# The node matrix beside conv 1's node product, and a new order of the steps, in a two-layer graph network

## The chip, the cores and the metric

The kernel runs on one core of a Trainium2 chip. The metric is device time in microseconds for the whole program, the median of several runs. One execution of it was profiled; times below in the form "at 1212.13 us" are counted from that execution's first instruction. The engines are PE (TensorE), DVE (VectorE), ACT (ScalarE), POOL (GpSimd) and SP (SyncE, which here only issues transfers).

## The reference

There are 128 graphs of 128 nodes with 512 features. Each goes through two layers, each with a layer norm and relu ahead and a residual sum behind.

```python
h = relu(layernorm(x))
# layer 0: two hypergraph convolutions with the same graph
H = (adj != 0); w = adj[0, :]
conv(h, W, b) = Dinv * (H @ (Binv * (H.T @ (h @ W.T)))) + b    # D = H @ w, B = H.sum(0)
r = layer_norm(relu(conv(h, W1, b1)))                         # 512 -> 1024
x = x + conv(r, W2, b2) + h                                    # 1024 -> 512
# layer 1: mean aggregation
h = relu(layernorm(x))
agg = (adj @ h) / max(adj.sum(-1), 1e-6)
x = x + relu(concat(h, agg) @ W.T)
```

## The kernel before

**Tiling.** One graph fills the 128 partitions with its nodes, so a graph is the unit of work. H (B^-1) H^T is a 128 x 128 matrix of the graph alone, the *node matrix*; it is made once and used in both convolutions. It comes from one matmul with 258 columns (`node_matrix`, L428 to L433, into `ps_s`): the columns hold H^T scaled by the high and by the low part of B^-1, and two columns more for D. ACT copies the first half out with a factor (L432), and DVE adds the second half (`node_sum`, L436 to L438). The result is `s`.

**Split products.** The weight products run as fp32r matmuls on operands split in high, low and difference parts. `product` (L521 to L537) opens two PSUM banks, a main one for high and low, and one for the difference: 12 matmuls of 512 columns for 512 inputs (8 and 4), 24 for 1024. Per graph that is `conv1_weights` for each half of the 1024 outputs (`rm`, `rd`, 24 in all), `conv2_weights` (`gm`, `gd`, 24), `layer1_mean` (`bm`, `bd`, 12) and `layer1_self` (`am`, `ad`, 12). With conv 2's node product (`conv2_nodes`, `ym`, `yd`, 3) and `aggregate` (3 into `am`, `ad`) this makes 78 matmuls of 512 columns a graph. Conv 1's node product (`conv1_nodes`, L485 to L489, into `pz`) is in plain fp32: four products of 128 columns, which show as eight matmuls.

**What lies between the products.** ACT writes the high part of each split operand and the main results; DVE writes low and difference parts, adds the difference results, and does all 32 x 32 block transposes. Full transposes go through DRAM: `inner_out` and `inner_in` write conv 1's normalised result `r` (512 KB) and read it back in blocks, four transfers; `inner_turn` transposes the blocks on DVE. `layer1_trip_out`, `layer1_trip_in`, `layer1_turn` do that for layer 1's input, `mean_out`, `mean_in`, `mean_transpose` for the scaled adjacency matrix.

**Order.** The whole order is written out by hand: `head()` for the first graphs, `step(s)` (L856 to L943) for s = 3 to 124, `tail()` for the rest. A step works on eight graphs at once, from `load_adjb` of graph s + 3 and `incidence` of s + 2 to `finish` and `store` of s - 4. Each engine takes its instructions in this order, and so does SP with its transfers; semaphores make an instruction wait for what it reads and for the buffer that it writes. A step on PE is: `node_matrix(s + 1)`, `conv1_weights(s, 1)`, `conv2_nodes(s - 2)`, `layer1_mean(s - 3)`, `conv1_nodes(s + 1)`, `layer1_self(s - 3)`, `conv2_weights(s - 1)`, `aggregate(s - 3)`, `conv1_weights(s + 1, 0)`.

**Stages.** The decorator `stage` (L115 to L124) drops a call whose graph lies outside 0 to 127, or which the set `done` already holds. So calls in `tail()` that were made earlier vanish.

**Buffers.** Most SBUF tags have one buffer, and several tags are shared: `t1` by the turned `r`, its difference part and conv 2's node parts; `t2` by the blocks read back and the low part; `t3` by the high part and conv 2's `gp`; `r` by conv 1's result of one graph after the other, which `inner_out` still reads; `junk` by `inner_spread`'s waste and by the output `o`, which `store` reads; `adj` by one graph's adjacency matrix, which `mean_out` reads. Six PSUM banks turn among the weight products, conv 2's node product and the like (`bank`), and two among `ps_s` and `pz` (`small_bank`, L109). The matrices `s` have four buffers.

**Lines that the steps below touch:** small scalings run on the engine that the call names, through `scaled` (L296 to L300: L298 on ACT, L300 on DVE and POOL); sums and differences through `combine` (L76 to L81), on POOL in halves of 256 columns; layer norms through `sums`, `spread`, `scales`, `shifts`, `normalise` (L304 to L326) under the names `x_...`, `inner_...`, `layer1_...`. `conv1_out` is L555, `inner_turn` and `layer1_turn` are L591, all high parts L612, all difference parts L621, `conv2_main` L690, `conv2_weights_out` L694, `conv2_high` L706, `node_high` L717, `conv2_out` L754, `layer1_self_out` L838, `finish` L844 (L847 for the last graphs), `store` L853.

## Time and profile before

| what | value |
|---|---|
| median of 3 runs | 2447.64 us (2446.86 to 2447.76) |
| the profiled execution's own time | 2447.67 us |
| its span, first to last instruction | 2445.9 us |
| granted TensorE clock | full (1.0) |
| PE matmul busy, instructions | 2422.7 us, 11170 |
| DVE busy, instructions | 2298.1 us, 5843 |
| ACT busy, instructions | 2009.9 us, 4512 |
| POOL busy, instructions | 1324.8 us, 1808 |
| DMA | 311.39 MB, mean 127 GB/s |
| spacing of node matrices on PE, steady steps | median 18.747 us |

A group's line gives the source line, the engine and operation, what it writes from what, how often, its busy time and mean length, and the idle time of its engine just before it with what ended it. A matmul's end is modelled and overlaps the next one's start, so on PE starts are compared. Instructions on DVE and ACT overlap their neighbours a little too, so the distance from start to start is some 80 or 100 ns less than a length.

### The profile page before, as it was taken

How to read it: one execution, taken by the hardware profiler on the slowest of the kernel's cores; microseconds unless marked ns; L12 is line 12 of the kernel's file. 1: busy time of each engine (PE TensorE's matmuls, PEld its weight loads, DVE VectorE, ACT ScalarE, POOL GpSimd, SP SyncE). 2: the span in 40 equal slices, each digit the busy share in tenths (PEclk: the TensorE clock that was granted, in tenths of full speed). 3: DMA queues.
4: the chain of work that ended last, by engine and by line, in shares of the span. 5: the costliest groups of instructions: out<-in, count | busy, mean ns of one | idle time of the engine just before them, and what ended most of it. 6: DMA issues, size and time to landing. Idle time of an engine off the chain costs nothing.

```text
span 2445.9 us, 41647 instructions
## 1 busy us (share of the span) xinstructions
PE 2422.7 (99%) x11170; PEld 2009.6 (82%) x11170; DVE 2298.1 (94%) x5843; ACT 2009.9 (82%) x4512; POOL 1324.8 (54%) x1808
## 2 busy tenths in 40 slices
PE   7999999999999999999999999999999999999998
PEld 5788888888888888888888888888888888888886
DVE  8899999999999999999999999999999999999987
ACT  8888888888888888888888888888888888888785
POOL 5555555555555555555555555555555555555552
PEclk9999999999999999999999999999999999999999
DMA  6344433344434443444344443434343444344432
GB/s 186 114 129 125 130 124 129 124 130 128 129 119 130 132 126 123 129 129 127 124 128 128 126 129 123 132 123 130 122 133 121 130 127 131 119 131 131 127 124 92
DMA packets 408956, 311.39 MB, mean 127 GB/s; under 512 B 176656, under 2 KB 339984, under 8 KB 408720
## 3 DMA queue, kind: packets, MB, share of 16 engines
q1 hardware_dynamic: 407888, 308.66, 40.1%
q8 instruction: 88, 1.44, 0.2%
q14 instruction: 148, 1.21, 0.2%
q10 hardware_dynamic: 576, 0.07, 0.0%
q0 software_dynamic: 256, 0.01, 0.0%
HBM read 166.21 MB, written 142.34 MB: 126 GB/s over the span
## 4 chain that ended last, share of the span: by engine, by line
PE 95%; ACT 2%; DVE 1%; DMA 1%; issue 1%; SPq 0%; POOL 0%; POOLq 0%; DVEq 0%; ACTq 0%
PE gm L530 19%; PE rm L530 18%; PE am L530 9%; PE bm L530 9%; PE gd L535 9%; PE rd L535 9%; PE bd L535 5%; PE ad L535 5%; PE pz L488 4%; PE am L832 2%; PE ad L832 1%; PE ym L743 1%; PE yd L744 1%; PE ym L742 1%; PE ps_s L430 1%
## 5 line engine op out<-in xcount | busy, mean ns | idle before, releaser
L306 ACT ACTIVATE h<-x_t 128x512 f32<-128x512 f32 x255 | 159.1, 624 | 291.8 <-DVE x_t L754 283.8
L81 POOL TENSOR_TENSOR r<-r,b_bc 128x256 f32<-128x256 f32 x500 | 358.7, 739 | 70.1 <-DVE r L555 54.4
L300 POOL TENSOR_SCALAR st<-st 128x1 f32<-128x1 f32 x130 | 82.3, 633 | 569.9 <-DVE st L317 563.2
L81 POOL TENSOR_TENSOR hl<-ht,hh 128x256 fp32r<-128x256 f32 x250 | 235.4, 963 | 216.5 <-ACT hh L612 216.5
L81 POOL TENSOR_TENSOR x_t<-x_t,h 128x256 f32<-128x256 f32 x256 | 239.8, 959 | 1.3 <-ACT h L326 1.1
L81 POOL TENSOR_TENSOR g<-g,c 128x256 f32<-128x256 f32 x246 | 177.6, 743 | 72.4 <-DVE g L694 72.4
L326 ACT ACTIVATE h<-x_t,st 128x512 f32<-128x512 f32 x255 | 206.1, 808 | 2.0 <-POOL st L300 1.2
L555 DVE SCALAR_TENSOR_TENSOR r<-rd,dinv,r 128x512 f32<-128x512 f32 x256 | 190.8, 746 | 7.7 <-ACT r L550 6.3
L81 POOL TENSOR_TENSOR x_t<-x_t,b_bc 128x256 f32<-128x256 f32 x256 | 187.2, 752 | 0.0
L311 ACT ACTIVATE h<-x_t,st 128x512 f32<-128x512 f32 x255 | 182.9, 717 | 4.1
L550 ACT ACTIVATE r<-rm,dinv 128x512 f32<-128x512 f32 x256 | 174.7, 684 | 7.7 <-PE rm L530 4.4
L694 DVE SCALAR_TENSOR_TENSOR g<-gd,g 128x512 f32<-128x512 f32 x127 | 87.8, 691 | 79.5 <-issue 70.4
L621 DVE SCALAR_TENSOR_TENSOR nd<-nh,nl 128x1024 fp32r<-128x1024 f32 x127 | 155.5, 1225 | 4.2
L326 ACT ACTIVATE r<-r,st 128x1024 f32<-128x1024 f32 x128 | 157.8, 1233 | 0.1
L591 DVE STREAM_TRANSPOSE nt<-nb 128x1024 f32<-128x1024 f32 x127 | 156.9, 1235 | 0.4 <-DMA nb<-n_scratch 0.3
L81 DVE TENSOR_TENSOR nl<-nt,nh 128x1024 fp32r<-128x1024 f32 x127 | 153.5, 1208 | 1.9 <-ACT nh L612 1.7
L530 PE MATMUL am<-w31h,hh 128*128 128x512 f32 x504 | 146.8, 413 | 0.0
L311 ACT ACTIVATE junk<-r,st 128x1024 bf16<-128x1024 f32 x128 | 145.2, 1134 | 0.1
L488 PEld LDWEIGHTS pz<-s,h 128*128 128x128 f32 x1024 | 134.5, 192 | 11.1 <-ACT h L326 0.7
L530 PE MATMUL rm<-w11h,z 128*128 128x512 f32 x512 | 140.3, 396 | 0.0
L530 PE MATMUL rm<-w11l,z 128*128 128x512 f32 x512 | 139.3, 393 | 0.0
L530 PE MATMUL rm<-w10h,z 128*128 128x512 f32 x512 | 138.2, 392 | 0.9 <-ACT z L501 0.9
(244 smaller groups left out, 7594.1 us busy)
## 6 DMA issues: line engine op xcount, KB each, us to landing
n_scratch<-r SPq DMA_DIRECT2D x128, 512.0 KB, 2.6
nb<-n_scratch SPq DMA_DIRECT2D x508, 128.0 KB, 2.8
x_t<-in_x_dram SPq DMA_DIRECT2D x128, 256.0 KB, 2.7
h_scratch<-h SPq DMA_DIRECT2D x127, 256.0 KB, 2.3
hb<-h_scratch SPq DMA_DIRECT2D x508, 64.0 KB, 1.9
out_dram<-o SPq DMA_DIRECT2D x127, 256.0 KB, 2.0
adj_t<-in_adj_dram SPq DMA_DIRECT2D x128, 64.0 KB, 1.9
an_scratch<-adj_t SPq DMA_DIRECT2D x128, 64.0 KB, 1.6
```

The lines of the kernel that those rows point to most:

```text
L81: eng.tensor_tensor(dst[:, s], a[:, s], b[:, s], op)
L306: copy(junk, src, func, accum_out=t[:, 0:1])
L311: copy(junk, src, AF.Square, bias=t[:, 1:2], accum_out=t[:, 2:3])
L326: copy(dst, src, func, bias=t[:, 5:6], scale=t[:, 4:5])
L488: nc.tensor.matmul(z[:, k * P : (k + 1) * P], H0[g][:, k * P : (k + 1) * P], S[g], start=True, stop=True)
L530: nc.tensor.matmul(pm, left[i](k), right(i, k), start=(i == 0 and k == 0), stop=(i == 1 and k == kk - 1))
L535: nc.tensor.matmul(pd, left[2](k), right(2, k), start=(k == 0), stop=(k == kk - 1), skip_group_check=True)
L550: copy(R[g][:, HALVES[half]], PY.pop((g, half)), AF.Copy, scale=DN[g][:, 1:2])
L555: nc.vector.scalar_tensor_tensor(r, PR.pop((g, half)), dn[:, 0:1], r, MUL, ADD)
L591: nc.vector.transpose(nt.rearrange("p k (i b) -> p k i b", b=B), t.rearrange("p i k a -> p k i a"))
L621: nc.vector.scalar_tensor_tensor(t, h, 2.0**-12, low, MUL, SUB)
L694: nc.vector.scalar_tensor_tensor(G[g], PG.pop(g), 4096.0, G[g], MUL, ADD)
```

## The change

`node_matrix` becomes a thin stage around a plain function `matrix`. For graphs 4 to 125 `conv1_nodes(g)` calls `matrix(g + 1)` ahead of its own matmuls, and marks that stage as done; the call of `node_matrix` is gone from `step`, and the one for graph 126 in `tail` vanishes. In step s, `conv1_nodes(s + 1)` so makes the matrix of graph s + 2, one graph earlier than before; `node_sum` moves to s + 2 with it. The stages of `step` come in a new order. PE's is now: `conv1_weights(s, 1)`, `conv2_nodes(s - 2)`, `layer1_mean(s - 3)`, `layer1_self(s - 3)`, then the matrix of s + 2 and `conv1_nodes(s + 1)`, `conv2_weights(s - 1)`, `aggregate(s - 3)`, `conv1_weights(s + 1, 0)`. SP's is: `inner_out`, `mean_out`, `load_adj`, `inner_in`, `mean_in`, `store`, `layer1_trip_out`, `load_adjb`, `load_x`, `layer1_trip_in`. Some stages change their engine: `node_floor`, `conv1_bias(s, 0)` and `shifts(s, 2)` go from POOL to DVE; `incidence_weight`, `incidence_scale(s + 2, 1)` and `shifts(s + 2, 1)` from DVE to ACT; `incidence_scale(s + 2, 0)` and `mean_scale` from DVE to POOL. `head` and `tail` are unchanged.

```diff
--- before.py
+++ after.py
@@ -424,8 +424,7 @@
         c = SPLIT["sb", g][i]
         scaled(eng, SB[g][:, i * (P + 1) : i * (P + 1) + P], HT[g], c)
 
-    @stage
-    def node_matrix(g):
+    def matrix(g):
         PS[g] = ps = small_bank("ps_s")
         nc.tensor.matmul(ps[:, : 2 * P + 2], HT.pop(g), SB.pop(g)[:, : 2 * P + 2], start=True, stop=True)
         s = small.tile([P, P + 1], FP, tag="s", name="s", bufs=4)
@@ -433,6 +432,10 @@
         S[g] = s
 
     @stage
+    def node_matrix(g):
+        matrix(g)
+
+    @stage
     def node_sum(g):
         s = S[g]
         nc.vector.scalar_tensor_tensor(s, PS.pop(g)[:, P + 1 : 2 * P + 2], 4096.0 if steady(g) else 1.0, s, MUL, ADD)
@@ -483,6 +486,9 @@
 
     @stage
     def conv1_nodes(g):
+        if 4 <= g <= N - 3:
+            done.add((node_matrix.f, g + 1))
+            matrix(g + 1)
         PZ[g] = z = small_bank("pz")
         for k in range(KD):
             nc.tensor.matmul(z[:, k * P : (k + 1) * P], H0[g][:, k * P : (k + 1) * P], S[g],
@@ -854,93 +860,92 @@
 
 
     def step(s):
+        incidence(s + 2)
+        conv2_bias(s - 2)
+        inner_out(s - 1)
         node_high(s - 2)
-        conv2_bias(s - 2)
+        conv1_weights(s, 1)
+        mean_out(s - 3)
+        layer1_high(s - 3)
+        node_rest(s - 2)
         conv2_high(s - 2)
+        incidence_count(s + 2, nc.vector)
+        conv1_main(s, 0)
+        incidence_weight(s + 2, nc.scalar)
+        node_floor(s + 1, nc.vector)
+        load_adj(s - 2)
         layer1_self_main(s - 4)
-        layer1_high(s - 3)
-        inner_out(s - 1)
+        inner_in(s - 1)
+        x_norm(s + 1)
+        incidence_inverse(s + 2)
         conv2_low(s - 2, nc.vector)
-        x_norm(s + 1)
-        node_rest(s - 2)
-        conv1_main(s, 0)
+        conv1_out(s, 0)
+        conv2_rest(s - 2)
+        layer1_low(s - 3)
+        conv2_nodes(s - 2)
+        conv1_main(s, 1)
+        layer1_rest(s - 3)
+        conv2_out(s - 2)
+        incidence_high(s + 2)
+        layer1_sums(s - 2)
+        layer1_mean(s - 3)
+        mean_in(s - 3)
+        conv1_bias(s, 0, nc.vector)
+        layer1_mean_main(s - 3)
+        conv1_out(s, 1)
+        incidence_scale(s + 2, 1, nc.scalar)
+        inner_turn(s - 1)
+        layer1_spread(s - 2)
+        inner_high(s - 1)
         layer1_self_out(s - 4)
-        conv2_rest(s - 2)
-        node_matrix(s + 1)
-        conv1_weights(s, 1)
-        conv1_out(s, 0)
-        mean_out(s - 3)
-        layer1_low(s - 3)
-        layer1_rest(s - 3)
-        inner_in(s - 1)
-        conv2_nodes(s - 2)
-        node_sum(s + 1)
-        node_floor(s + 1, nc.gpsimd)
-        conv2_out(s - 2)
-        conv1_main(s, 1)
-        conv1_out(s, 1)
-        inner_turn(s - 1)
-        layer1_sums(s - 2)
-        mean_in(s - 3)
-        layer1_spread(s - 2)
-        conv1_bias(s, 0)
-        load_adj(s - 2)
-        incidence(s + 2)
-        layer1_mean(s - 3)
-        incidence_weight(s + 2, nc.vector)
         scales(s - 2, 3)
-        layer1_mean_main(s - 3)
+        mean_transpose(s - 3)
+        shifts(s - 2, 3, nc.vector)
         finish(s - 4)
+        incidence_scale(s + 2, 0, nc.gpsimd)
+        layer1_mean_out(s - 3)
+        layer1_norm(s - 2)
+        inner_low(s - 1, nc.vector)
+        layer1_self(s - 3)
+        store(s - 4)
+        mean_operator(s - 2)
+        layer1_trip_out(s - 2)
         conv1_bias(s, 1)
-        shifts(s - 2, 3, nc.vector)
+        inner_rest(s - 1)
         conv1_nodes(s + 1)
-        store(s - 4)
+        inner_sums(s)
+        conv2_weights(s - 1)
+        load_adjb(s + 3)
+        conv1_high(s + 1)
+        layer1_mean_high(s - 3)
+        layer1_mean_low(s - 3, nc.vector)
+        residual(s + 1)
+        mean_rest(s - 3)
+        mean_degree(s - 2, nc.vector)
+        inner_spread(s)
+        conv2_main(s - 1)
+        node_scale(s + 1)
+        scales(s, 2)
+        mean_inverse(s - 2)
+        shifts(s, 2, nc.vector)
+        layer1_mean_rest(s - 3)
+        node_up(s + 1, nc.vector)
+        conv1_low(s + 1)
+        conv1_rest(s + 1)
         load_x(s + 2)
-        inner_high(s - 1)
-        conv1_high(s + 1)
-        mean_transpose(s - 3)
-        layer1_mean_out(s - 3)
-        layer1_self(s - 3)
-        mean_operator(s - 2)
-        inner_low(s - 1, nc.vector)
-        inner_rest(s - 1)
-        layer1_norm(s - 2)
-        inner_sums(s)
-        layer1_mean_high(s - 3)
-        inner_spread(s)
-        conv2_weights(s - 1)
-        layer1_mean_low(s - 3, nc.vector)
-        node_scale(s + 1)
-        mean_rest(s - 3)
-        layer1_trip_out(s - 2)
+        node_sum(s + 2)
+        inner_norm(s)
+        layer1_trip_in(s - 2)
         x_sums(s + 2)
-        incidence_count(s + 2, nc.vector)
-        mean_degree(s - 2, nc.vector)
-        conv2_main(s - 1)
-        scales(s, 2)
-        layer1_mean_rest(s - 3)
-        layer1_trip_in(s - 2)
-        conv1_low(s + 1)
-        incidence_inverse(s + 2)
-        residual(s + 1)
-        mean_inverse(s - 2)
         conv2_weights_out(s - 1)
-        conv1_rest(s + 1)
-        shifts(s, 2, nc.gpsimd)
-        load_adjb(s + 3)
-        inner_norm(s)
-        incidence_high(s + 2)
+        aggregate(s - 3)
         layer1_turn(s - 2)
         x_spread(s + 2)
-        aggregate(s - 3)
-        mean_scale(s - 2, nc.vector)
-        incidence_scale(s + 2, 0, nc.vector)
         scales(s + 2, 1)
+        shifts(s + 2, 1, nc.scalar)
         conv1_weights(s + 1, 0)
-        incidence_scale(s + 2, 1, nc.vector)
-        shifts(s + 2, 1, nc.vector)
+        mean_scale(s - 2, nc.gpsimd)
         residual_bias(s + 1)
-        node_up(s + 1, nc.vector)
 
     def head():
         load_w1(0, 0)
```

## The prediction

> **What bounds the kernel now.** I read the shares of busy time first, then the chain that ended last, then the order of work on PE inside one step, and last the waits of the other engines.
>
> ```profile
> PE 2422.7 (99%) x11170; PEld 2009.6 (82%) x11170; DVE 2298.1 (94%) x5843; ACT 2009.9 (82%) x4512; POOL 1324.8 (54%) x1808
> ...
> PE 95%; ACT 2%; DVE 1%; DMA 1%; issue 1%; SPq 0%; POOL 0%; POOLq 0%; DVEq 0%; ACTq 0%
> ```
>
> The chain is PE nearly throughout. A PE row's end is modelled, so I go by starts. The timeline of PE in one steady step (start, length, op):
>
> ```profile
> 1209.41 1.07 PE L530 MATMUL rm<-w10h,z 128*128 128x512 f32 x4
> 1210.32 1.07 PE L530 MATMUL rm<-w10l,z 128*128 128x512 f32 x4
> 1211.23 1.07 PE L535 MATMUL rd<-w10d,z 128*128 128x512 f32 x4
> 1212.13 0.28 PE L430 MATMUL ps_s<-sb,adjt 128*128 128x258 f32 x1
> 1212.25 1.09 PE L530 MATMUL rm<-w11h,z 128*128 128x512 f32 x4
> 1213.18 1.09 PE L530 MATMUL rm<-w11l,z 128*128 128x512 f32 x4
> 1214.10 1.07 PE L535 MATMUL rd<-w11d,z 128*128 128x512 f32 x4
> 1215.02 0.39 PE L742 MATMUL ym<-gp,sp 128*128 128x512 f32 x1
> ...
> 1217.51 1.07 PE L535 MATMUL bd<-w30d,hd 128*128 128x512 f32 x4
> 1218.42 1.05 PE L488 MATMUL pz<-s,h 128*128 128x128 f32 x8
> 1219.22 1.17 PE L530 MATMUL am<-w31h,hh 128*128 128x512 f32 x4
> 1220.23 1.07 PE L530 MATMUL am<-w31l,hl 128*128 128x512 f32 x4
> ```
>
> Undisturbed, twelve 512-column matmuls take 1212.13 - 1209.41 = 2.72 us, 0.2267 each. Those after the node matrix take 1215.02 - 1212.13 = 2.89 with it, so the node matrix costs 0.17, not the 0.12 to the next start. The starts of single matmuls over 102 steady steps give the split: 121.7 ns to the next start (median 118), then nine matmuls of 224 to 236 ns, 41.3 too many in sum (I call this the recovery), and 7.4 on average for which the node matrix itself starts late. The node product pz costs 1220.23 - 1218.42 - 0.907 = 0.90: spacings of 108 to 112 ns, and a recovery of 16.5 ns spread over only three matmuls. Together: 78 x 0.2267 + 0.170 + 0.906 = 18.756 us, which is the mean spacing of node matrices; the median is 18.747. So PE has no idle time to remove. Only the 0.17 can change.
>
> Who else is near PE's period (waits by engine over the whole span: total, times, longest):
>
> ```profile
> POOL st L300 <- DVE st L317: 563.2, 125, 5.2
> ACT h L306 <- DVE x_t L754: 283.8, 118, 2.7
> ...
> DVE g L694 <- issue: 70.4, 117, 0.6
> ...
> ACT gp L706 <- POOL g L81: 68.2, 117, 1.1
> ```
>
> POOL waits 4.5 us a step at shifts and ACT 2.4 at layer1_sums: both have room. DVE stands still 0.6 us a step, until conv 2's difference product is done (L694; the order says so, the view names no releaser). That is all the room it has.
>
> **What the Trainium skill says.** *TensorE: Matmul & The Clock Gate*, section "LDWEIGHTS (loading the stationary operand)": a load takes about its columns over 1.2 GHz, here an estimate of 107 ns. The trace agrees: pz keeps a spacing of 112 ns, where loads follow each other without a gap. *PSUM — Partial Sum Buffer*, "Engine vs sequencer instructions": ACT, DVE and POOL queues are strict FIFO, so one waiting instruction holds all behind it; the 0.6 us above is such a wait. *SBUF — State Buffer*, "Who interferes with whom": a DVE instruction with two SBUF inputs contends with a POOL instruction that reads SBUF, and who came first holds the ports. The trace agrees: finish (L844) takes 1022 ns at the median while POOL adds x_t and h, and 648 ns at the least in the tail's form of it.
>
> **The change part by part.**
>
> *PE.* 122 node matrices (graphs 5 to 126) move from between conv 1's two weight products to just ahead of pz. No matmul is added or dropped. The spacing from node matrix to the first pz is not in the trace. Lower bound 112 (the spacing of loads), upper 122 (today's mean); I take 118, the median. Today the first pz spacing is 108, later 112: +4 ns. The recovery of 41.3: pz runs at the pace of the loads, so the state after its eight matmuls should not depend on what stood ahead, and the 16.5 after pz is paid anyway; I take 0 for it. From both sides: a node matrix at 40.3 us recovered with 10 ns, one at 57.5 us, whose inputs had been ready for 3 us, still paid 42, so readiness is not its cause and it might survive: 0 to 41. The late start (7.4): today DVE scales end 0.36 us ahead of the node matrix; in the new order ACT and POOL scale some 2 us ahead of it: gone. Sum: -3.7 - 41.3 - 7.4 + 4 = -48.4 ns, a period of 18.708. Times 122: **-5.9 us**. No cover is needed, PE being the path.
>
> *Work moved between engines.* DVE takes conv1_bias(s,0) (0.60), shifts(s,2) (0.12), node_floor (0.06) and gives away mean_scale (0.16), two incidence_scale (0.20 each), shifts(s+2,1) (0.12), incidence_weight (0.07): +0.03 us. (DVE instructions overlap their neighbours by about 80 ns, ACT's by 100; these are start to start.) ACT gets 0.30 + 0.18 + 0.10 (L298 takes 396 ns on 128x128 and 280 on one column of st, in head and tail) and reaches about 16 of 18.7 us. POOL loses some 1.3 us (1478 + 646 + 212 ns away, two scales of about 0.61 to it). So only the order counts.
>
> *The order.* I set PE's times at zero where conv1_weights(s,1) starts: products for ym 2.72, bm 3.40, am 6.12, node matrix 8.84, pz 8.96, gm 9.87, aggregate 15.31, the next rm 15.99, the next step 18.71. The tight turn goes from one conv2_out to the next, start to start from before's rows. DVE: conv2_out 1.53, incidence_high 0.25, conv1_bias 0.60, conv1_out 0.65, inner_turn 1.16, layer1_self_out 0.60, scales, mean_transpose, shifts 0.42, finish 0.96, layer1_mean_out 0.58, inner_low 1.13, mean_operator 0.19, inner_rest 1.16, layer1_mean_low 0.61, mean_rest 0.41, mean_degree 0.06, node_scale 0.27, scales, mean_inverse, shifts 0.39: 10.97. Then ACT, which waits for these shifts: inner_norm 1.14, x_sums 0.97, x_spread 1.13: 3.24. DVE scales(s+2,1) with both handovers 0.25. ACT: shifts 0.18, node_high 0.20, layer1_high 0.52, conv2_high 0.67: 1.57. DVE, held at conv2_low until then: conv2_low 0.62, conv1_out 0.67, conv2_rest 0.65, layer1_rest 0.62: 2.56. Sum **18.59** against PE's 18.71: it closes with 0.12 to spare. The stall at conv2_low (some 0.4 us, with the end of x_spread 0.1 more) replaces today's at L694. Behind it stand conv2_rest, for which PE's yd waits (due at 21.88; done at 21.1), and layer1_rest.
>
> Two terms of it can move. finish holds 0.33 of port contention, which goes if POOL's first half of residual is over by then (they come within 0.1 us of each other); conv2_low now meets layer1_low on POOL, up to 0.33. So the turn is 18.3 to 18.9. A second one, ym to inner_low to gm's low part: conv2_out starts at 3.38, inner_low 6.75 later, 1.2 long: 11.36, PE's load for it at 11.45. 0.1 to spare.
>
> *Transfers.* SP passes load_adj ahead of inner_in and load_adjb, load_x ahead of layer1_trip_in. inner_norm ends at 15.55, so inner_out is issued at 15.6 rather than 16.6, and mean_out (mean_scale on POOL, done by 15) right after. load_adj waits for mean_out's landing, at most 2.3 us, under inner_out's own 2.6 to 3.4. inner_in's last block lands some 5.0 us after its first issue, 5.4 in the next step, for inner_turn at 6.4: 1.0 to spare, against 0.3 today (landed 5.31, used 5.62). layer1_trip_in lands at 16.0 for a use at 16.9, x at 14.8 for 15.5, store frees junk at 11.7 for 12.0. Cost nothing; if one lands later by more than this, the turn above pays it.
>
> **The rivals.**
>
> *A, forecast, 0.56:* PE stays the bound: 2447.67 - 5.9 = **2441.8**. The sum is made against the profiled execution (2447.67, span 2445.9, 1.8 around it); the median of the runs, 2447.64, is the same within 0.03. Its own range, 2440 to 2444, takes in the spacing (+-0.7) and a microsecond or two at head and tail, which meet another order.
>
> *B, slower, 0.31:* the turn through conv2_low doesn't close. Its place: conv2_high on ACT behind shifts, node_high and layer1_high, conv2_low on DVE behind that. Price: finish keeps its 0.33 and conv2_low pays another 0.33, 18.59 + 0.33 = 18.92 a step, or 18.92 - 18.756 = 0.16 over today's, times 122: +20, **2467.5**; it decides from a turn of 18.76. For it: DVE at 94% and ACT laden with 0.6 us more. Against it: conv2_low finds POOL between its halves as likely as not. If it overshoots less, the time lies between.
>
> *C, the recovery moves along, 0.13:* the 41 ns come after gm's first matmuls instead: only 3.7 + 7.4 - 4 = 7 ns are saved, 0.9 us: **2446.8**. For it: the row at 57.5 us.
>
> **How the numbers follow.** A measurement of this kernel tells about 0.2% from no change: 2442.8 and 2452.6 are the bounds. A gives 0.47 faster, 0.09 same; B 0.30 slower, 0.01 same; C 0.11 same, 0.02 faster. Faster 0.49, same 0.21, slower 0.30. The range goes from 2440.2 (below A's own low end little is left, 0.03) to 2465, beyond which lies nearly half of B (0.15).
>
> **What would show it.** Right: node matrix to node matrix 18.71; pz 0.12 after the node matrix; after pz three slightly long matmuls, and conv 1's second half in 2.72 us. DVE's standing time at gp (L81) rather than L694. Wrong: PE with gaps ahead of ym (L742) or of gm with w20l, or ACT h L306 waiting longer for x_t; nine long matmuls after pz would be C; inner_turn waiting for nb would mean that transfers, not engines, set the turn.

## The result, and the profile after

The changed kernel takes 2455.94 us (median of 5 runs, 2455.58 to 2460.47) against 2447.64 (2446.86 to 2448.07) for the kernel before on the same chip: a ratio of 1.0037, 95% interval 1.0026 to 1.0048. It is slower by 8 us where 6 us less were forecast. The profiled execution of the changed kernel took 2455.84 us, its span is 2454.1 us.

Shares of busy time and the chain that ended last, changed kernel. Lines behind the change are 6 higher than in the kernel before (yd L744 is now L750).

```profile
PE 2426.1 (99%) x11170; PEld 2008.4 (82%) x11170; DVE 2286.1 (93%) x5598; ACT 2091.6 (85%) x4878; POOL 1249.1 (51%) x1565
...
PE 89%; ACT 4%; DMA 2%; DVE 2%; issue 1%; SPq 0%; ACTq 0%; POOL 0%; POOLq 0%; DVEq 0%
```

The chain was PE for 95% before; now ACT, DVE and DMA hold 8% of it, where they held 4%. Busy shares hardly moved and wouldn't have told this.

Timeline of PE in one step in which nothing is late (start, length, op), changed kernel:

```profile
1138.54 1.07 PE L536 MATMUL rm<-w10h,z 128*128 128x512 f32 x4
...
1149.20 1.07 PE L541 MATMUL ad<-w31d,hd 128*128 128x512 f32 x4
1150.11 0.28 PE L429 MATMUL ps_s<-sb,adjt 128*128 128x258 f32 x1
1150.22 1.05 PE L494 MATMUL pz<-s,h 128*128 128x128 f32 x8
1151.03 1.17 PE L536 MATMUL gm<-w20h,nh 128*128 128x512 f32 x4
1152.04 1.08 PE L536 MATMUL gm<-w21h,nh 128*128 128x512 f32 x4
1152.96 1.08 PE L536 MATMUL gm<-w20l,nl 128*128 128x512 f32 x4
1153.88 1.07 PE L536 MATMUL gm<-w21l,nl 128*128 128x512 f32 x4
1154.79 1.07 PE L541 MATMUL gd<-w20d,nd 128*128 128x512 f32 x4
...
1157.28 0.39 PE L536 MATMUL rm<-w10h,z 128*128 128x512 f32 x1
```

The merged stage is there: node matrix (L429) and node product (L494) stand 0.12 us apart, and conv 1's second half now runs in the plain 2.72 us (from 1141.27 to 1143.98 in the same view). But the groups behind pz are long: 1.01, 0.92, 0.92, 0.91 us from start to start, against 1.01, 0.91, 0.91 in the kernel before. Over four groups, by unrounded starts, that is 126 ns more than 4 x 0.907 at the median, against 97 before: 29 ns more are paid behind pz, where the 41 ns of recovery behind the node matrix went. The undisturbed step (median spacing of the first rm of a graph, graphs 8 to 119) is 18.733 us, against 18.747: 14 ns saved, not 48.

So undisturbed steps are shorter, and still the kernel is longer. The loss lies in single steps. I call a step late when it exceeds the median by more than 0.1 us. Among graphs 8 to 119 the kernel before has 4 late steps, the changed kernel 24 (0.15 to 1.35 us each). They exceed the median by 0.97 us together before and by 11.36 after. Over all 112 steps, with those that fall short of the median subtracted, it is 1.03 and 11.14; I call this the net excess. 10.1 more of it less 112 x 0.014 = 1.6 makes +8.5; the spans differ by 8.2, and head and tail hold the rest.

The view of waits (total us, times, longest), first of the kernel before, then of the changed one:

```profile
DVE ht L591 <- DMA hb<-h_scratch: 3.1, 4, 1.4
ACT r L550 <- DMA n_scratch<-r: 2.4, 6, 0.7
...
ACT h L306 <- DMA x_t<-in_x_dram: 1.5, 1, 1.5
```

```profile
DVE gp L81 <- ACT gp L712: 30.8, 118, 0.3
...
PEld yd L750 <- ACT h L326: 14.0, 23, 1.1
...
DVE ht L597 <- DMA hb<-h_scratch: 12.4, 18, 1.3
...
ACT h L306 <- DMA x_t<-in_x_dram: 9.4, 12, 1.6
...
PE yd L750 <- DVE sp L737: 5.2, 13, 0.9
ACT junk L311 <- DMA out_dram<-o: 5.2, 8, 1.1
...
ACT r L556 <- DMA n_scratch<-r: 4.1, 4, 1.3
```

Three things stand in it. DVE waits at conv2_low in every step, 0.26 us, in the place that was forecast (some 0.4 there). TensorE's weight load for yd waits in 23 steps (the named ACT instruction had long been done; the row of PE names conv2_rest, DVE L737). And waits for transfers have grown: for hb from 4 to 18, for x from 1 to 12, and for the store (out_dram) from none to 8; those for n_scratch went from 6 to 4, but are longer. Every one of the 24 late steps has such a wait in it or at the end of the step ahead: 13 follow x or hb (6.2 us together), 7 the store (2.3), 4 n_scratch (2.8). The longest is graph 116, which starts at 2191.40. Timelines of ACT, DVE and PE (in brackets the idle time ahead of the instruction and what ended it):

```profile
2192.39 0.63 ACT L306 ACTIVATE h<-x_t 128x512 f32<-128x512 f32 x1 [1.56 <-DMA x_t<-in_x_dram]
...
2195.68 0.62 ACT L712 ACTIVATE gp<-g 128x512 fp32r<-128x512 f32 x1
```

```profile
2193.09 0.71 DVE L597 STREAM_TRANSPOSE ht<-hb 128x512 f32<-128x512 f32 x1 [0.96 <-DMA hb<-h_scratch]
...
2196.32 0.81 DVE L81 TENSOR_TENSOR gp<-g,gp 128x512 fp32r<-128x512 f32 x1 [0.26 <-ACT gp L712]
2197.06 0.74 DVE L561 SCALAR_TENSOR_TENSOR r<-rd,dinv,r 128x512 f32<-128x512 f32 x1
2197.72 0.68 DVE L737 SCALAR_TENSOR_TENSOR sp<-gp 128x512 fp32r<-128x512 f32 x1
```

```profile
2198.54 0.47 PE L750 MATMUL yd<-sp 128*128 128x512 f32 x1 [0.85 <-DVE sp L737]
```

x lands late, ACT stands 1.56 us at x_sums, everything behind it on ACT's queue is late up to conv2_high, DVE's conv2_low and conv2_rest follow, and PE stands still at yd. Nothing on ACT's queue passed the waiting instruction.

Why was x late? The DMA view for 12 us around it (first the queues, then the median time from issue to landing):

```profile
q8 instruction: 1, 0.02, 0.6%
q14 instruction: 1, 0.01, 0.2%
...
x_t<-in_x_dram SPq DMA_DIRECT2D x1, 256.0 KB, 4.8
hb<-h_scratch SPq DMA_DIRECT2D x4, 64.0 KB, 3.8
```

The same view one step earlier, where nothing is late:

```profile
q14 instruction: 1, 0.01, 0.4%
...
x_t<-in_x_dram SPq DMA_DIRECT2D x1, 256.0 KB, 2.6
hb<-h_scratch SPq DMA_DIRECT2D x4, 64.0 KB, 2.4
```

On q8 one packet of 16 KB passes, a block of instructions. Ahead of graph 116 it ran from 2189.55 to 2190.70, with x and hb in flight. Such packets take 1.08 us at the median (0.88 to 1.74), 77 of them in steps 8 to 119, one about every 27 us. Counted over all transfers of those steps: 159 land more than 0.6 us (up to 2.4) above the median of their kind; 138 of these overlapped a q8 packet, 20 one of 8 KB on q14, one neither; of 1886 transfers that overlapped none, one was late. In the kernel before, 146 are late (up to 1.8), 98 with q8, 37 with q14, 11 with neither. So the disturbance was there before. But it isn't the same for the four transfers that are waited for. Those over 0.6 us late, and the latest landing, of x: 7 and 1.4 us before, 13 and 2.1 after; of the last part of hb: 11 and 1.2, 9 and 1.3; of n_scratch: 11 and 1.0, 9 and 2.4; of the store: none (0.4 at most), 7 and 2.0. The Trainium skill, *DMA: Bandwidth & Descriptors*, "Queues, rings and completion order", says that a DMA engine goes round its queues packet by packet and drains a whole packet before it switches; the trace fits this in part: a packet takes 0.88 to 1.74 us and a landing is up to 2.4 us late, somewhat more than one packet. No run shows which of the engines a packet passes.

What differs besides, for x, hb and the store, is the room. I measured two distances, both as medians over steps. First, from a transfer's last landing to the instruction that waits for it. Second, from the end of conv2_rest (DVE's sp<-gp) to the start of PE's weight load for yd in undisturbed steps, less 0.116, which is what this distance is where yd waits in every step (swap, turn_short and hb_x_own below).

| us | x | hb | store | n_scratch | operand of yd |
|---|---|---|---|---|---|
| before | 1.67 | 0.98 | 1.30 | 0.82 | 0.885 |
| after | 0.49 | 0.37 | 0.90 | 1.04 | 0.223 |

A late hb could be 0.98 + 0.885 late before PE stood still; now it is 0.37 + 0.223 = 0.59. For x it is 2.55 and 0.71. (Without any spare an instruction starts some 0.12 after the landing, so all of the first kind are about 0.1 smaller in use.) An estimate of what room alone does to x and hb: what their landings exceed these sums by, taken over steps 8 to 119, is nothing in either kernel with the room of before. With the room of after it is some 7 us for the landings of before, and some 8 for those of after, where 6.2 were lost. For n_scratch the room at the wait has not shrunk, so there the later landings count, or the smaller room of the operand; no run separates these. Timelines of the kernel before, DVE and PE's loads, and then of the changed kernel, show the second distance:

```profile
1213.52 0.73 DVE L731 SCALAR_TENSOR_TENSOR sp<-gp 128x512 fp32r<-128x512 f32 x1
```

```profile
1215.24 0.19 PEld L744 LDWEIGHTS yd<-sp 128*128 128x128 f32 x1
```

```profile
1143.20 0.67 DVE L737 SCALAR_TENSOR_TENSOR sp<-gp 128x512 fp32r<-128x512 f32 x1
```

```profile
1144.21 0.19 PEld L750 LDWEIGHTS yd<-sp 128*128 128x128 f32 x1
```

Before: 1213.52 + 0.73 = 1214.25, then 0.99 to the load. After: 1143.87, then 0.34.

### The profile page after: what moved, and what is told of

Read it like the earlier page. It is cut to its first block, busy times and chain, and to the rows that moved or that the text cites. A ratio compares the mean times of both kernels' runs of the same rounds, so it can differ in the third digit from the quotient of the medians.

```text
span 2454.1 us, 41654 instructions
## 1 busy us (share of the span) xinstructions
PE 2426.1 (99%) x11170; PEld 2008.4 (82%) x11170; DVE 2286.1 (93%) x5598; ACT 2091.6 (85%) x4878; POOL 1249.1 (51%) x1565
## 4 chain that ended last, share of the span: by engine, by line
PE 89%; ACT 4%; DMA 2%; DVE 2%; issue 1%; SPq 0%; ACTq 0%; POOL 0%; POOLq 0%; DVEq 0%
PE gm L536 18%; PE rm L536 17%; PE bm L536 9%; PE am L536 9%; PE gd L541 8%; PE rd L541 8%; PE bd L541 4%; PE ad L541 4%; PE pz L494 4%; PE am L838 2%; PE yd L750 1%; PE ad L838 1%; PE ym L749 1%; PE ym L748 1%; DMA x_t<-in_x_dram 1%
## 5 line engine op out<-in xcount | busy, mean ns | idle before, releaser
L300 POOL TENSOR_SCALAR adj_t<-adj_t,deg 128x128 f32<-128x128 f32 x125 | 137.0, 1096 | 547.4 <-issue 541.5
L81 POOL TENSOR_TENSOR r<-r,b_bc 128x256 f32<-128x256 f32 x256 | 184.3, 742 | 320.2 <-DVE r L561 308.2
L300 POOL TENSOR_SCALAR sb<-adjt,sb 128x128 fp32r<-128x128 f32 x124 | 75.5, 609 | 150.3 <-ACT sb L418 149.2
L536 PE MATMUL gm<-w20h,nh 128*128 128x512 f32 x508 | 148.4, 414 | 0.1
L536 PE MATMUL gm<-w21h,nh 128*128 128x512 f32 x508 | 137.1, 392 | 0.0
L536 PE MATMUL bm<-w30h,hh 128*128 128x512 f32 x504 | 136.7, 393 | 0.3 <-ACT w30d L201 0.2
```

Source lines behind the costliest of these rows:

```text
L81: eng.tensor_tensor(dst[:, s], a[:, s], b[:, s], op)
L300: eng.tensor_scalar(dst, src, c, None, MUL)
L536: nc.tensor.matmul(pm, left[i](k), right(i, k), start=(i == 0 and k == 0), stop=(i == 1 and k == kk - 1))
```

## The experiments

All are edits of the changed kernel. The ratio is against the kernel before, on the same chip. "Operand" is the second distance above.

| kernel | median us | ratio, 95% interval | undisturbed step | operand | late steps; net excess, us |
|---|---|---|---|---|---|
| after | 2455.94 | 1.0026 to 1.0048 | 18.733 | 0.223 | 24, 11.1 |
| shift | 2472.97 (one run) | | 18.733 | 0.223 | 25, 12.8 |
| o_own | 2458.09 | 1.0023 to 1.0049 | 18.733 | 0.223 | 26, 13.8 |
| r_halves | 2459.05 | 1.0026 to 1.0056 | 18.733 | 0.222 | 26, 14.0 |
| x_early | 2454.99 | 1.0016 to 1.0035 | 18.733 | 0.223 | 22, 9.9 |
| bias_pool | 2457.35 | 1.0026 to 1.0051 | 18.734 | 0.220 | 28, 13.4 |
| bias_x | 2453.39 | 1.0015 to 1.0033 | 18.733 | 0.221 | 18, 8.5 |
| bias_x_own | 2453.35 | 1.0013 to 1.0031 | 18.733 | 0.221 | 20, 9.1 |
| turn_long | 2467.95 | 1.0065 to 1.0090 | 18.733 | 0.037 | 30, 20.7 |
| swap | 2466.36 | 1.0056 to 1.0086 | 18.760 | 0 | 33, 15.8 |
| hb_x_own | 2473.21 | 1.0088 to 1.0122 | 18.920 | 0 | 17, 5.1 |
| rest_first | 2489.75 | 1.0156 to 1.0184 | 18.947 | 0.103 | 32, 20.3 |
| turn_short | 2506.42 | 1.0219 to 1.0247 | 19.100 | 0 | 34, 16.3 |

Late steps are those of one profiled execution; kernels that differ by 2 or 3 us in them should not be ranked by it. The kernel before took between 2447.4 and 2449.4 us on the chips used, so that medians of different rows compare less well than ratios.

**Does an earlier issue of the transfers give the loss back?** Three edits together (room), the first of them alone (sp_early), the other two each alone (o_own, r_halves).

```diff
         layer1_trip_out(s - 2)
+        load_x(s + 2)
+        layer1_trip_in(s - 2)
+        load_adjb(s + 3)
...
-        load_adjb(s + 3)
...
-        load_x(s + 2)
...
-        layer1_trip_in(s - 2)
```

```diff
-        spread((2, g), R[g], pool.tile([P, DH], mybir.dt.bfloat16, tag="junk", name="junk"), DH)
+        p, tag = (left, "h1") if 3 <= g <= N - 4 else (pool, "junk")
+        spread((2, g), R[g], p.tile([P, DH], mybir.dt.bfloat16, tag=tag, name="junk"), DH)
```

```diff
-        NT[g] = trip_out(R.pop(g), "n")
+        r = R.pop(g)
+        NT[g] = d = dram.tile([P, DH], FP, tag="nd", name="n_scratch")
+        for c in HALVES:
+            nc.sync.dma_start(out=d[:, c], in_=r[:, c])
```

Expected of the three together: 

> The changed kernel with room given back to three transfers, nothing else: SP issues load_x and layer1_trip_in right behind layer1_trip_out (load_adjb last), inner_spread's waste goes to another buffer so that it needn't wait for store, and inner_out goes out in two halves so that conv1_main waits for the first half alone. Theory 1 (late landings): the 11.1 us of 24 late steps (steps 8 to 119) are steps whose x, hb, out or n_scratch transfer landed 0.6 to 2.3 us late; with room they vanish, 2445.3 us (2444.3 to 2447.5), under 5 late steps. Theory 2 (the turn of DVE, ACT and POOL, or the merged stage, is too long by itself): transfers don't matter, 2455 to 2457.

Of the first alone: 

> Only SP's order: load_x and layer1_trip_in ahead of load_adjb. Theory 1: thirteen late steps (6.2 us) follow a late x or hb; they go, 2449.7 us (2448.5 to 2451.5); those behind store and inner_out stay. Theory 2: 2455 to 2457.

Of the second: 

> Only inner_spread's waste in another buffer, so that store's landing frees nothing that is waited for. Theory 1: six or seven late steps (2.3 us) follow a late store; they go, 2453.5 us (2452.5 to 2455). Theory 2: 2455 to 2457.

Of the third: 

> Only inner_out in two transfers of half the columns. Theory 1: four late steps (2.8 us) follow a late n_scratch, for which conv1_main waits before it overwrites r; the first half lands some 0.6 us or more before today's whole, 2453.2 us (2452 to 2455). Against it: SP is busy 0.4 us longer a step, which could make load_adj and inner_in late. Theory 2: 2455 to 2457.

Measured: room 2514.98 (1.0260 to 1.0291), sp_early 2509.40 (1.0227 to 1.0261), o_own 2458.09, r_halves 2459.05. All missed. The order of SP's queue is no free choice: SP issues in order too. sp_early, waits of SP's queue, then of DVE:

```profile
SPq L590 <- DMA h_scratch<-h: 158.4, 124, 1.8
SPq L590 <- DVE anp L376: 142.8, 115, 1.3
```

```profile
DVE raw L390 <- DMA adjb<-in_adj_dram: 65.7, 114, 7.3
```

Put ahead, the trip back of h waits on SP for its buffer and for h's landing, and the adjacency behind it lands late in 114 steps. With the changed order load_adjb and load_x rightly pass it. o_own and r_halves gave nothing: one packet delays much of what is in flight (138 of the 239 transfers that overlapped one were late), so where one waiter is freed, the next one is late. In o_own no late step follows the store any more, but 22 (11.4 us) follow x or hb, for 13 (6.2 us). The first half of n_scratch, at its latest, was late by as much as the whole (4.46 us for a median of 2.04).

**Is it the instruction packets?** 32 more fill matmuls in the head shift the block boundaries of PE's program against the graphs; nothing in a step changes.

```diff
         fill(768)
+        for _ in range(32):
+            fill(32)
```

> 32 fill matmuls of 32 columns more in the head, which show as 64 weight loads and 64 matmuls: half of one 16 KB block of PE's instructions[...]. Nothing else changes. If late landings come from the fetch of such blocks over the same DMA engines, the late steps fall on other graphs than 9, 12, 22, 25, 28, 32, 35, 41, 45, 48, 58, 67, 77, 80, 90, 93, 106, 109, 113, 116 (at least half of them elsewhere), as many and as long in sum (8 to 15 us in steps 8 to 119). If they come from the data or the memory, they stay on these graphs.

Measured: 2472.97 us, of which the longer head holds 13.6. Step and operand as in the changed kernel; 25 late steps, a net excess of 12.8 us, at other graphs, but for one, than in the changed kernel (11, 14, 17, 19, 20, 30, ... for 9, 12, 22, 25, 27, 28, ...). The number stays, the places move, as was expected if the blocks are the cause. Together with the count of overlaps above this shows the packets to be what makes transfers late.

**Which part of the change does it: the merge or the order?** The new order with the node matrix back between the products (order_alone), and the merged stage with the node matrix last (swap):

```diff
     def conv1_nodes(g):
-        if 4 <= g <= N - 3:
-            done.add((node_matrix.f, g + 1))
-            matrix(g + 1)
...
-        conv1_weights(s, 1)
...
         incidence_weight(s + 2, nc.scalar)
-        node_floor(s + 1, nc.vector)
+        node_matrix(s + 1)
+        conv1_weights(s, 1)
...
         conv2_out(s - 2)
+        node_sum(s + 1)
+        node_floor(s + 1, nc.vector)
...
-        node_sum(s + 2)
```

```diff
             done.add((node_matrix.f, g + 1))
-            matrix(g + 1)
         PZ[g] = z = small_bank("pz")
...
+        if 4 <= g <= N - 3:
+            matrix(g + 1)
```

> The new order of the steps without the merged stage: node_matrix(s + 1) stands between conv 1's two weight products again, as before the change, its ACT copy after incidence_weight, node_sum and node_floor after conv2_out. Theory 1 (the order leaves too little room for late transfers): late steps as in the changed kernel, 20 to 30 of them, 2456 to 2459 us, undisturbed period 18.747. Rival (the merged stage costs the time, the order is harmless): back to 2447 to 2449, few late steps.

> The merged stage with its two parts exchanged: pz first, then the node matrix, then gm. On the recovery after short matmuls. If it is a debt of the short matmuls together, whichever comes last: undisturbed period 18.733 as now. If it is fixed by the last short matmul: the 41 ns of a node matrix with a weight product behind it, against some 28 to 33 measured behind pz now: 18.74 to 18.75, total up 1 to 2 us. Late steps as now in both.

Measured: order_alone 2556.80 (1.0417 to 1.0452), a step of 19.723. It tells nothing of the order by itself, since a new wait covers it, that of the next incidence for the one buffer that the node matrix reads:

```profile
DVE adjt L393 <- PE ps_s L429: 87.6, 113, 1.1
```

Merge and order hang together: the new order begins a step with the incidence, and needs the matrix to be made a graph earlier. order_alone does bear on the recovery, though. With gm behind pz and no node matrix ahead, the same four groups are 113 ns over 4 x 0.907 at the median, 97 or less in a quarter of the undisturbed steps and 123 or more in another quarter; in the changed kernel a quarter stays at 101 or less. So the 29 ns cannot be put down to the node matrix alone. swap: 2466.36, which is 9 more above the kernel before than the changed kernel is, where 0 to 2 was expected. On PE the stretch from the start of the pair to gm's fourth group behind it is 21 ns shorter than in the changed kernel (3.752 for 3.773). But ACT now waits for the node matrix ("ACT s L431 <- PE ps_s L429", 34.0 us in 120 times), conv2_high starts 2.97 us after the step's start for 2.61, the operand's 0.22 us are used up, and the step is 18.760: here the turn binds, as rival B has it.

**Room for x alone:**

```diff
         layer1_trip_out(s - 2)
+        load_x(s + 2)
...
-        load_x(s + 2)
```

> Only load_x(s + 2) moves, ahead of the four load_adjb, so that x is issued 2 us earlier and layer1_trip_in is as late as now. Theory 1: steps late by x alone (12, 25, 64, 93, 106, 119 in the profiled run, about 2.8 us) go and those late by x and hb shrink; 2452.3 us (2450.5 to 2454.5), late steps 14 to 20. Theory 2 (the turn is too long by itself): 2455 to 2457.

Measured: 2454.99 (10 runs), 0.5 above the expected range. But the kernel before took 2449.02 on this chip, 1.4 more than on the first: it is +6.0 for the changed kernel's +8.3, so 2.3 us of the 3.6 expected, with intervals that overlap. x's room grew from 0.49 to 2.34, and no late step begins with x any more; those that begin with hb (0.42), the store and n_scratch stay.

**Is it paid on the way from the landing to yd?** turn_short takes 0.3 us out of ACT's run ahead of conv2_high, turn_long puts 0.2 in.

```diff
-        node_high(s - 2)
...
-        layer1_high(s - 3)
...
         x_sums(s + 2)
+        node_high(s - 1)
         x_spread(s + 2)
         scales(s + 2, 1)
+        layer1_high(s - 2)
         shifts(s + 2, 1, nc.scalar)
```

```diff
+    pad = const.tile([P, 2], FP, name="pad")
...
+        copy(pad[:, 0:1], eps, AF.Copy)
+        copy(pad[:, 1:2], eps, AF.Copy)
         node_high(s - 2)
```

> Of the changed kernel, on ACT only: the high part of the node matrix (three instructions) goes into the step before, between the sums of x and the spread of x, and the high part of layer 1 goes there ahead of the shifts; both come out of the run of ACT work that begins a turn, so that the turn through conv 2's low part begins some 0.3 us sooner. Theory (a late transfer is paid only beyond what the turn through conv2_low has to spare, 0.24 us): the undisturbed period stays 18.73 us, since PE sets it; each late step costs about 0.34 us less, and the excess of the late steps falls from 11.1 to some 4.5 us: 2449.3 us (2448 to 2452). Rival (what counts is the room of the transfer itself, and a shorter turn doesn't give it any): 2455 to 2457, as the changed kernel.

> Of the changed kernel, with two more 128x1 copies on ACT ahead of the node matrix's high part (0.1 us each), in the run of ACT work that begins a turn; they compute nothing that is used. Theory (late transfers are paid beyond what the turn has to spare): the spare of an undisturbed step falls from 0.24 to some 0.04 us, the undisturbed period stays 18.73 to 18.75 us, each late step costs 0.2 us more and there are more of them: 2461 us (2459 to 2466). Rival (a transfer's own room counts): unchanged, 2455 to 2457. If the turn already bound the undisturbed steps, the period itself would grow by 0.2 us: 2481.

And the shorter run, the earlier x and the waste of its own together: 

> Three edits of the changed kernel together: the shorter turn on ACT, the load of x issued ahead of the load of the adjacency, and the waste of the output's spread in a tile of its own rather than in that which the store reads. Theory: with some 0.6 us to spare in the turn and more room for x and the store, few late landings are left to pay for; the undisturbed period stays 18.73 us: 2447.5 us (2446.5 to 2450), about the time before the change. Rival (late landings cost the same wherever room is made, since one fetch delays all that is in flight): 2453 to 2456.

turn_long: 2467.95. Its step, timelines of DVE and PE's loads:

```profile
1150.05 0.67 DVE L738 SCALAR_TENSOR_TENSOR sp<-gp 128x512 fp32r<-128x512 f32 x1
```

```profile
1150.87 0.19 PEld L751 LDWEIGHTS yd<-sp 128*128 128x128 f32 x1
```

1150.72 to 1150.87: the operand's room is down to 0.15 - 0.116 = 0.04. The undisturbed step is 18.733 to the nanosecond, and the late steps go from 24 to 30, the net excess from 11.1 to 20.7 us. But the room at the waits shrank too, of hb from 0.37 to 0.21 and of x from 0.49 to 0.35. So a late hb or x has about 0.33 less in all, and it is these steps that grew, from 13 with 6.2 us to 19 with 15.8; those behind the store and n_scratch stayed at 5. The direction is the theory's, and a time that stays as it was is out. Whether the room of the operand or that of the transfer costs more, this run doesn't separate, so the rival isn't refuted by it. The size is 10.3 us by the kernel before on the same chip (9.5 of it net excess), for an expected 5: 13 steps of 0.33 us give an estimated 4.3, the rest is other landings than in the changed kernel, among them some that had been absorbed.

turn_short: 2506.42, and short_room 2493.56 (1.0166 to 1.0194), not the 2449 and 2447.5 expected. conv2_high did come 0.29 us sooner. But DVE's rows that write sp, changed kernel first, turn_short second (minimum, median and maximum in ns):

```profile
L729 DVE SCALAR_TENSOR_TENSOR sp<-sp,s x118: 284/287/294, 104.8 to 2308.6; 128x128 fp32r<-128x128 f32 x118
L730 DVE SCALAR_TENSOR_TENSOR sp<-sp,s x118: 281/284/288, 105.0 to 2308.8; 128x128 fp32r<-128x128 f32 x118
```

```profile
L729 DVE SCALAR_TENSOR_TENSOR sp<-sp,s x118: 285/816/893, 105.1 to 2357.1; 128x128 fp32r<-128x128 f32 x118
L730 DVE SCALAR_TENSOR_TENSOR sp<-sp,s x118: 818/825/844, 105.7 to 2357.7; 128x128 fp32r<-128x128 f32 x118
```

The earlier high part lets POOL start layer1_low earlier, beside node_rest (in one step POOL from 1145.25 to 1146.74, DVE from 1145.38 to 1146.88), and two instructions of 0.28 take 0.82. The operand is done 0.65 later instead of sooner, more than its room, and the step grows by 0.37 to 19.10: now rival B's mechanism, the turn as the bound, is there in full. The Trainium skill, *SBUF — State Buffer*, "Who interferes with whom", names this case (two SBUF inputs on VectorE beside a GpSimd instruction that reads SBUF, one waits for the whole of the other); the measured 0.54 each agrees.

**Does room elsewhere on VectorE help?**

```diff
-        conv1_bias(s, 0, nc.vector)
...
         incidence_scale(s + 2, 0, nc.gpsimd)
+        conv1_bias(s, 0)
```

> Of the changed kernel, the first half of conv 1's bias goes from VectorE back to GpSimd, behind its scaling of the incidence, where GpSimd idles for some 2.7 us: one VectorE instruction of 0.68 us leaves the turn through conv2_low, two of 0.74 us come on GpSimd, beside VectorE instructions that read PSUM. Nothing on TensorE changes. Theory (a late transfer is paid only beyond what the turn has to spare, and the turn is VectorE's work in one period): the spare grows from 0.24 to some 0.8 us, the undisturbed period stays 18.733 us, and of the late steps' 11.1 us only what exceeds 0.6 us in a step is left, some 2 us: 2446.7 us (2445.5 to 2450). Rival 1 (what counts is the transfer's own room): 2455 to 2457, as the changed kernel. Rival 2 (GpSimd beside VectorE lengthens the turn by more than the 0.68 us that it loses, as the shorter turn on ACT did): the period itself grows, over 2460.

> As the first half of the bias on GpSimd, and the load of x issued ahead of the load of the adjacency. Theory: the spare of the turn and the earlier x together leave 1 to 2 us of late steps; 2446 us (2445 to 2449). Rivals as for the bias alone: 2453 to 2455 if only the transfer's own room counts, over 2460 if GpSimd lengthens the turn.

> As the one before, and the waste of the output's spread in a tile of its own. Theory: 2445.5 us (2444.5 to 2449), the undisturbed period times its steps with hardly a late one. Rivals as for the bias alone: 2453 to 2456, or over 2460.

Measured: 2457.35, 2453.39, 2453.35. The theory as I had put it, that any of DVE's time in a step is room, falls. The bias stands behind conv2_out, and is not on the way from a landing to yd: operand 0.220, as without it, and these waits are nearly those of the changed kernel:

```profile
DVE gp L81 <- ACT gp L712: 30.2, 115, 0.3
PEld yd L750 <- ACT h L326: 15.8, 25, 1.1
```

Freed time on DVE did not reach the operand. And it isn't a clean test: the waits came sooner against the landings, and the room of hb fell from 0.37 to 0.27, of x from 0.49 to 0.33, of the store from 0.90 to 0.56. bias_x and bias_x_own lie in the ranges of the rival by which the transfer's own room counts. They are the fastest of all edits, still 5.7 us above the kernel before: in bias_x 5 late steps (1.8 us) follow x or hb, but 9 (5.7 us) follow n_scratch.

**Shortening that way on VectorE itself**, by an exchange of two instructions, alone, with the earlier x, and with the waste of its own:

```diff
-        conv1_out(s, 0)
         conv2_rest(s - 2)
+        conv1_out(s, 0)
```

> Of the changed kernel, two VectorE instructions change places: the difference part of conv 2's operand (conv2_rest, 0.68 us), for which TensorE's last small matmul waits in every late step, comes ahead of the first half of conv 1's output (conv1_out, 0.74 us). No work is added or moved to another engine. Theory as it stands after the bias runs (a late landing is handed on along ACT's and VectorE's order to that matmul, whose operand is ready only 0.24 us before its slot; room elsewhere on VectorE is not on this path): the operand is ready 0.74 us sooner, about 1 us before its slot, the undisturbed period stays 18.733 us, the late steps' sum falls from 11.1 to 2 or 3 us: 2447.5 us (2446 to 2451). Rival 1 (the transfer's own room counts): unchanged, 2455 to 2457. Rival 2 (the turn itself, from one x_t through ACT to the next, has no more to spare, so that what doesn't stop this matmul stops another one later): late steps stay at 7 to 11 us with another waiter, 2452 to 2456.

> The same exchange on VectorE, and the load of x issued ahead of the load of the adjacency. Theory: 2446.5 us (2445.5 to 2450). Rival 1: 2453 to 2455, as the earlier x alone. Rival 2: 2451 to 2455.

> The same, and the waste of the output's spread in a tile of its own, so that ACT doesn't wait for the store. Theory: 2446 us (2445 to 2449.5), at or below the time before the change. Rival 1: 2453 to 2455. Rival 2: 2451 to 2455.

Measured: 2489.75, 2484.64 (1.0137 to 1.0165), 2482.74 (1.0128 to 1.0156). All missed. rest_first, the row of conv2_rest and a new wait:

```profile
L737 DVE SCALAR_TENSOR_TENSOR sp<-gp x118: 1107/1112/1119, 106.6 to 2344.9; 128x512 fp32r<-128x512 f32 x118
```

```profile
PEld bm L536 <- DVE r L561: 38.9, 116, 0.4
```

Brought forward, conv2_rest runs into POOL's layer1_low (1112 ns for 675), and conv1_out, now behind it, frees its PSUM bank too late for bm, which waits 0.33 in every step. The theory isn't refuted by this, the edit didn't make the room.

**Room at the waiting places, with the way left alone:**

```diff
-        incidence(s + 2)
...
+        load_x(s + 2)
         load_adjb(s + 3)
...
-        load_x(s + 2)
...
+        incidence(s + 3)
         layer1_turn(s - 2)
...
         head()
+        incidence(5)
```

(and the waste of its own, as above).

> Of the changed kernel, with three waits for transfers each given room and nothing that shortens the path behind them: on VectorE the two instructions of the next incidence (0.31 and 0.29 us) come ahead of the transposition of hb, so that this is wanted some 0.6 us later; the load of x is issued ahead of the load of the adjacency; the waste of the output's spread has a tile of its own. The wait for the store of n_scratch stays as it is. Theory (a late landing costs what it exceeds its own room and the path's 0.24 us by): the late steps that begin with hb, x or the output's store go, those of n_scratch stay, some 5 us of the 11; undisturbed period 18.733 us: 2450 us (2448.5 to 2453). Rival 1 (the next transfer behind binds at once, as with the earlier x): 2453 to 2455. Rival 2 (moved VectorE work meets GpSimd's, as in three runs before): the period grows, over 2458.

Measured: 2473.21. Late steps fall to 17 and the net excess to 5.1 us, the 5 expected to stay, and hb's room is 1.13. But the step is 18.920. DVE now answers ACT's x_spread later, and ACT's node_high comes late for DVE:

```profile
ACT st L298 <- DVE st L317: 88.0, 122, 1.1
DVE sp L730 <- ACT sp L724: 66.3, 118, 0.6
```

That lengthens the turn by more than its 0.22. The fall of the late steps proves little, since a step longer by 0.19 absorbs lateness by itself.

## Why the prediction was wrong

- **The step that failed** is "Cost nothing; if one lands later by more than this, the turn above pays it". Its second half is what happens. The first half was worked from median times to landing. The rooms it gave, 0.7 for x and 0.9 for hb, were too large (0.49 and 0.37); that for the store, 0.3, was too small (0.90), and it gave none for the n_scratch that conv1_main waits for. Above all, 159 of the transfers land 0.6 to 2.4 us above the median, and the prediction neither looked for that in the trace of before, where 146 land 0.6 to 1.8 above it, nor asked what room absorbed them there. Price: 10.1 us, of which about 6 behind x and hb.
- **The recovery, "I take 0 for it"**, was wrong as well: 29 ns more are paid behind pz, by a cause that stays open (order_alone). The upper bound, 41, was in the text, and rival C (7 ns saved) is the nearer reading: 14 ns are saved. This term cost 29 x 122 = 3.5 us of the 5.9. Two other terms hold: 119 ns from node matrix to pz for 118, the second half of conv 1 plain.
- **The turn of 18.59 against 18.71** was right in place and nearly in size: it has 0.22 to spare, 18.51. The contention at finish went (median 695 ns for 1022), that at conv2_low came (811 ns for 693), as the two movable terms said.
- **Rival B** gave the sign, and its place, conv2_high behind ACT's run, conv2_low and conv2_rest behind that, is where the loss is paid. Its mechanism isn't what happened: the turn closes in every undisturbed step, and the loss comes in 24 steps by late transfers. Where an edit lengthened the turn by more than its spare (swap, turn_short, hb_x_own), B did appear, with the step's growth.
- **What is shown and what isn't.** Shown: the packets make transfers late (overlap, shift), in both kernels; each of the 24 late steps follows a wait for a transfer, and graph 116 shows the way from the landing through ACT and DVE to yd; less room on that way, at the wait and at the operand together, costs 9.5 us at an unchanged step (turn_long). Not shown: how the loss divides between the two rooms and the later landings; for x and hb the estimate above puts it down to the room, for the 5 us behind the store and n_scratch it stays open, and so does why these land later. Nor that the change with the room of the kernel before would keep its 14 ns a step. No edit gave the operand more room without lengthening something else, so that the shortfall of room accounts for the loss is read from the trace, not from a run that takes it away.

## What to carry to other kernels

A schedule that keeps the bounding engine busy at the medians isn't yet closed: ask how late the latest landings of each transfer are (before the change 7 of 112 x and 11 of 112 hb came over 0.6 us late), read it off the trace that you have, and compare it with the room at the waiting instruction plus the room of what stands behind it in queue order. An order that trades such room (for hb 1.9 us for 0.6) for 14 ns a step lost here, though every step without a late transfer is faster. And where two engines share ports, work moved earlier is not free: see what the other engine does in the new place first.

## What was not expected of the hardware

- Blocks of instructions are fetched all through the run and delay data: 89 packets of 16 KB in the span on q8, 0.88 to 1.74 us each; of 239 transfers that overlapped one in steps 8 to 119, 138 landed 0.6 to 2.4 us late. The Trainium skill, *Trainium Architecture — The Big Picture*, "The software stack", gives 64 bytes for an instruction, which makes a block an estimated 256 of them; 89 blocks hold an estimated 22,784, about as many as the 22,340 matmuls and weight loads of PE.
- The slow matmuls behind short ones are no fixed price of what stood ahead: over four groups they are 97 ns behind pz in the kernel before, 126 behind node matrix and pz, 113 behind pz alone in order_alone, and 20 in swap, where the node matrix comes last.
- From the end of a DVE instruction to the start of a waiting weight load 0.116 us pass, in each kernel in which yd waits in every step (swap, turn_short, hb_x_own).
